# Moving checks, row loads and row sums within a two-stream graph network kernel

## The chip, the cores and the metric

One core of a Trainium2 chip. The metric is the device time of one launch in microseconds; three runs of the kernel before gave 1787.79, 1788.79 and 1789.32, median 1788.79.

## The reference

16 graphs of 1024 nodes with 128 features each. `adj` is a symmetric 0/1 matrix per graph. Two residual blocks follow each other: four layers of a gated graph network, then four layers of a graph convolution with a normalization over all graphs.

```python
h = relu(layernorm(x))
for i in range(4):                       # block 1, per graph
    m = einsum('bjn,bjd->bnd', adj, h @ weight[i])
    h = gru_cell(m, h, w_ih[i], w_hh[i], b_ih[i], b_hh[i])
x = x + h * mask[:, :, None]
h = relu(layernorm(x))
for i in range(4):                       # block 2
    h = relu(einsum('bnm,bmc->bnc', adj, h @ W[i]) + b[i])
    h = gamma[i] * (h - mean(h)) * rsqrt(var(h) + eps) + beta[i]   # over graphs and nodes
x = x + h
```

The fast path of the kernel is exact only if the low 16 bits of each element of `adj` are zero (an element then fits bf16). The kernel therefore looks at these bits of every row of `adj` and branches to a general path if any is set.

## The kernel before, in words

**Block 1.** Two streams, `sa` (even graphs) and `sb` (odd graphs), alternate. Their order is written out by hand: under a manual schedule each engine executes its instructions in the order in which the program gives them. `half_step(one, two)` does one layer of both halves of the work: the gates of stream `two` (`products`, `reset_gate`, `candidate`, `update_gate`, `less`, `mixed`, each for the node halves 0 and 1) and the aggregation of stream `one` (`agg_step`, 32 matmuls of 128x512 from 8 row tiles and a high and a low part of the features, `ghw`). In the gates, ScalarE computes `r` (L1011), VectorE applies it (L1012, L1013), ScalarE computes the tanh (L1016) and `z` (L1020), VectorE mixes (L1027 to L1034), and the result leaves by a block transpose (L720) and DMAs on SP's queue (L591) to come back as the next layer's features (L598). After the aggregation ScalarE copies the two banks of `pm` to `m` (L955); the next half step's second product reads `m`. A clock counts the half steps (the first is step 3). `at(n, place, go)` puts a piece of side work into an agenda, and `due(place)` runs it when step n reaches that place. Places stand in this order in a half step: `ins`, `start`, (gates of half 0) `beside0`, `mid`, (gates of half 1) `beside1`, `outs`, `gap`, `end`. `plan(n)` fills the agenda for a change of graphs that ends at step n: the tail of the old graph, and the load, sums, factors and blocks of the coming x (`next_load`, `next_sums`, ...).

**A change of graphs.** In its last layer a stream fetches the next adjacency, eight row tiles of 128x1024 f32 through four staging tiles that both streams share. `fetch` issues the loads of rows 0 to 3 on SP's queue (L572); `first_four` casts them to row tiles on GpSimd (L577); `last_four` glances at rows 0 to 3, then issues the loads of rows 4 to 7 into the same four tiles and casts these. A glance (L586) is a ScalarE copy of the low 16 bits with an accumulator output; a look (L610) is a VectorE maximum over the same bits. Stream `sa` looks at rows 4 to 7 at the start of the next step, ahead of the gates' VectorE work; stream `sb` glances at them in the next step's gap. A staging tile can be loaded again only when its cast and its glance or look are done. Stream `sa` changes at steps 8, 16, ..., 56, and `sb` one step later.

GpSimd also casts each row to bf16 for a DMA transpose (L615, L616) whose results go to DRAM as the transposed adjacency (L629), and issues the loads of x (L539) and the stores of the middle results (L752, L755). `mids` lets GpSimd wait for the first column of a step's new `h` (L1091) before these stores.

**Block 2.** Here a scheduler orders the instructions by its own costs and priorities. For each layer and graph, eight rows of the transposed adjacency come back (L1308), are widened to f32 by VectorE or ScalarE (L1311, L1313) and enter 32 matmuls (L524). Graph 0 of the later layers goes a different way: it aggregates features that are not normalized yet, and `raw_weights` adds the shift times the row sums of `adj[0]` (`degree`, a tile of 128x1024 in which each partition holds the same row). `row_sums` computes `degree` after graph 0 of the first layer with 16 products with a matrix of ones (L1407) and two copies (L1411).

Of the kernel before, what the change touches and what calls it, by code (L numbers as in the profile page):

```python
# [341 lines left out]
def exact_path(  # L342
# [39 lines left out]
    def tmp(name):  # L382
        return ps_t.tile([P, HALF], F32, tag="tmp", name=name)

    adjT_d = [dram.tile([NB, P, N], BF16, tag=f"adjT{b}", name=f"adjT_d{b}") for b in range(B)]
    xmid_d = [dram.tile([N, C], F32, tag=f"xmid{b}", name=f"xmid_d{b}") for b in range(B)]
    ymid_d = [dram.tile([P, N], F32, tag=f"ymid{b}", name=f"ymid_d{b}") for b in range(B)]
# [20 lines left out]
    nc.vector.memset(eps_t, EPS)  # L408
    ones = const.tile([P, 1], F32, tag="ones", name="ones")
    nc.vector.memset(ones, 1.0)  # L410
    low = const.tile([P, (B + 2) * NB], F32, tag="low", name="low")
    nc.vector.memset(low, 0.0)

# [119 lines left out]
    with ExitStack() as st:  # L533
# [46 lines left out]
        def glance(b, stage, js):  # L580

            junk = work.tile([P, N], BF16, tag="junk", name=f"junk{b}_{js[0]}", bufs=1)
            for j in js:
                lows = stage[j % 4].bitcast(U16).rearrange("p (n t) -> p n t", t=2)[:, :, 0]
                k = b * NB + j
                nc.scalar.activation(junk, lows, AF.Copy, accum_out=low[:, k : k + 1])  # L586

        def exchange_out(t, name, d=None):
            if d is None:
# [180 lines left out]
        class Stream:  # L770
# [54 lines left out]
            def plan(self, n, tail=None):  # L825

                if tail:
                    b, xt, hT, parts = tail
                    end = {}

                    def sums():
                        end["norm"] = tail_sums(b, xt, hT, parts)

                    def blocks(hf):
                        if hf == 0:
                            end["y"] = y_mid(b)
                        norm_blocks(xt, end["y"], end["norm"], range(hf * BH, (hf + 1) * BH))

                    at(n + 2, "gap", sums)
                    at(n + 3, "mid", lambda: store_xmid(b, xt))  # L840
                    at(n + 3, "gap", lambda: norm_factors(end["norm"]))
                    at(n + 4, "beside0", lambda: blocks(0))
                    at(n + 4, "beside1", lambda: blocks(1))
                    at(n + 5, "mid", lambda: store_ymid(b, end["y"]))
                if self.b + 2 < B:
                    at(n + 5, "mid", self.next_load)
                    at(n + 6, "start", self.next_sums)
                    at(n + 6, "gap", self.next_factors)
                    at(n + 7, "beside0", lambda: self.next_blocks(0))
                    at(n + 7, "beside1", lambda: self.next_blocks(1))  # L850
                    at(n + 7, "end", self.ins_away)

            def fetch(self):

                if self.i == 3 and self.b + 2 < B and not written[0]:
                    if self is sa:
                        t = turned_tile(f"stage{self.b + 2}").bitcast(F32)
                        room[0] = [t[:, 2 * q : 2 * q + 2, :].rearrange("p a n -> p (a n)") for q in range(4)]
                    self.stage = room[0]
                    stage_rows(self.b + 2, self.stage, range(4))  # L860

            def first_four(self):
                if self.stage:
# [2 lines left out]
            def last_four(self):  # L866
                if self.stage:
                    b, stage, self.stage = self.b + 2, self.stage, None
                    glance(b, stage, range(4))
                    stage_rows(b, stage, range(4, NB))  # L870
                    self.rows += round_rows(b, stage, range(4, NB))

                    def looks():
                        for j in range(4, NB):
                            look(b, stage[j % 4], j)

                    if self is sa:
                        at(clock[0] + 1, "start", looks)
                    else:
                        at(clock[0] + 1, "gap", lambda: glance(b, stage, range(4, NB)))  # L880

            def take(self):
                self.xt, self.y = self.next_x, self.next_y
# [175 lines left out]
        def at(n, place, go):  # L1059
            agenda.setdefault((n, place), []).append(go)  # L1060

        def due(place):
            for go in agenda.pop((clock[0], place), ()):
                go()

        def first_step(one, two, gated, halfway):

            feed.next_step()
            if one is sa:
                feed.jobs = transposes([(s.b, s.rows) for s in (sa, sb)])  # L1070
            one.split_step()
            feed.some(2)
            two.gate_step(0)
            two.half_away(0)
            if feed.full or (clock[0], "mid") in agenda:
                mids(two)
            feed.some(1)
            two.gate_step(1)
            two.half_away(1)
            gated()  # L1080
            one.agg_step(0)
            halfway()
            feed.some(NB if one is sa else 1)
            one.agg_step(1)
            two.finish()
            clock[0] += 1
# [8 lines left out]
        def half_step(one, two, gated=None, halfway=None):  # L1095

            feed.next_step()
            counts = (2, 1, 1)
            if one is sb and one.i == 0:
                feed.jobs = transposes([(s.b, s.rows) for s in (sa, sb)])  # L1100
                counts = (0, 0, 0)
            elif two is sb and two.i == 0:
                counts = (2, 2, 1)
            elif two is sa and two.i == 1 and two.across:
                counts = (3, 1, 1)
            due("ins")
            due("start")
            if one.i > 0:
                one.halves_back()
            else:  # L1110
                one.hw = hw_tiles(one.b, f"ghw{one.b}_0")
            two.fetch()
            feed.some(counts[0])
            two.products(0)
            two.reset_gate(0)
            due("beside0")
            two.candidate(0)
            two.less(0)
            one.high(0)
            two.update_gate(0)  # L1120
            one.low(0)
            two.mixed(0)
            two.half_away(0)
            two.first_four()
            if feed.full or (clock[0], "mid") in agenda:
                mids(two)
            one.high(1)
            feed.some(counts[1])
            two.products(1)
            two.reset_gate(1)  # L1130
            due("beside1")
            one.low(1)
            two.candidate(1)
            two.less(1)
            two.update_gate(1)
            two.last_four()
            two.mixed(1)
            two.half_away(1)
            due("outs")
            due("gap")  # L1140
            due("end")
            if gated:
                gated()
            one.agg_step(0)
            if halfway:
                halfway()
            feed.some(counts[2])
            one.agg_step(1)
            two.finish()
            clock[0] += 1  # L1150
# [4 lines left out]
        with tc.manual_schedule(engines=every):  # L1155
# [115 lines left out]

            sa.plan(0)
            sb.plan(1)
            first_step(sa, sb, looks, lambda: ahead(1))
            first_step(sb, sa, lambda: turn_ih(prep, w_g, 2), lambda: ahead(2))
            written[0] = False
# [122 lines left out]
            nc.tensor.matmul(pc[hf], w_c[:, i, :], mt[:, cols], start=True, stop=True)  # L1399
        conv_done(0, i, pc, stats)  # L1400

    def row_sums(rows):

        pd = [tmp(f"pt_deg{hf}") for hf in range(NH)]
        for j in range(NB):
            for hf in range(NH):
                nc.tensor.matmul(  # L1407
                    pd[hf], ones_r, rows[j][:, hf * HALF : (hf + 1) * HALF], start=(j == 0), stop=(j == NB - 1)
                )
        for hf in range(NH):  # L1410
            nc.scalar.copy(degree[:, hf * HALF : (hf + 1) * HALF], pd[hf])  # L1411

    xo = []

    def pieces(b):
# [28 lines left out]
            for n0, n in pieces(k):  # L1444
                nc.gpsimd.dma_start(xo_piece(k, n0, n), by_node(xmid_d[k], n0, n))

    ones_r = work.tile([P, P], F32R, tag="ones_r", name="ones_r", bufs=1)
    nc.vector.tensor_copy(ones_r, ones.to_broadcast([P, P]))
    degree = w_mT.rearrange("p l c -> p (l c)")[:, :N]

    stats = small.tile([P, B * NH, 6], F32, tag="bn_st", name="stats0")
# [1 line left out]
    for b in range(B):  # L1453
        rows = load_adjT(b, 0)
        hw_next = first_split(b + 1) if b + 1 < B else None
        pm = banks(b, 0)
        aggregate(pm, hw, rows, 0)
        if waiting:
            last = first_weights(*waiting, stats)
            if b == 1:  # L1460
                with tc.issue_after(last.ins):
                    sb.rest()
        if b == B - 1:
            hw_next = raw_split(1)
        aggregate(pm, hw, rows, 1)
        if b == 0:
            row_sums(rows)
        hw, waiting = hw_next, (b, pm)


# [112 lines left out]
```

## Time and profile before

| What | us |
|---|---|
| median of three runs | 1788.79 |
| profiled execution | 1789.26 |
| its span, first to last instruction | 1787.5 |
| TensorE busy | 1759.3 |
| VectorE busy | 1305.9 |
| ScalarE busy | 1107.6 |
| GpSimd busy | 379.3 |
| glances, 84 on ScalarE (L586) | 88.6 and 15.8 for the accumulator reads |
| looks at staged rows, 36 on VectorE (L610), one | 1.22 |
| row-sum products, 16 on TensorE (L1407) | 3.9 |
| ScalarE idle until `pm` is aggregated, before the copies to `m` | 163.5 |
| ScalarE idle until VectorE has `r`, before the tanh | 253.1 |

The granted clock of TensorE is 0.999. A line of the timeline has the start, the duration, engine, line of the kernel, operation, tiles (out<-in) and shape; "x2" means that two records are merged, and in brackets stands how long the engine sat idle before it and what ended that. A group's line has its count, busy time, mean ns of one and the idle time before it. Ends of matmuls are modelled; the distance of two starts is the sounder figure. Block 1 ends near 1166 us, block 2 near 1758.

### The profile page before, as it was taken

To read this page: it belongs to the slowest core of one execution; us is meant where nothing else is said; L and a number is where in the kernel's file an instruction comes from. 1 tells how busy PE (TensorE), PEld (TensorE's weight loads), DVE (VectorE), ACT (ScalarE), POOL (GpSimd) and SP (SyncE) were. 2 spreads that over 40 slices of the span, in tenths; PEclk is the share of its full clock that TensorE was granted. 3 is DMA by queue.
4 is the path that set the end of the run, shared out by engine and by line. 5 is a ranking of instruction groups with operands and counts; after the bars stand their busy time and mean duration, and the time that the engine had idled before them with its cause. 6 is when DMAs were issued, how large, how long until landed. Compare 5 with 4: busy or idle time off the path is not lost. (4 is left out here: it accounts for less than half of the span.)

```text
span 1787.5 us, 22335 instructions
## 1 busy us (share of the span) xinstructions
PE 1759.3 (98%) x6734; PEld 1191.7 (67%) x6734; DVE 1305.9 (73%) x2310; ACT 1107.6 (62%) x1713; POOL 379.3 (21%) x417
## 2 busy tenths in 40 slices
PE   9999999999999999999999999999999999999997
PEld 6565655565656565556555556577778888888886
DVE  7677877887887787887797787676666666666665
ACT  5356556556566556665655655476777767768765
POOL 4314323332331331422432333010100000000011
PEclk9999999999999999999999999999999999999999
DMA  7467657777676676776756768788766575767667
GB/s 259 135 175 262 189 163 272 179 208 241 204 200 213 223 212 197 245 202 202 260 169 186 265 174 227 256 287 311 271 228 241 207 253 201 245 224 245 238 217 268
DMA packets 363617, 400.16 MB, mean 224 GB/s; under 512 B 158188, under 2 KB 239888, under 8 KB 363488
## 3 DMA queue, kind: packets, MB, share of 16 engines
q1 hardware_dynamic: 342736, 323.59, 57.6%
q0 software_dynamic: 20224, 74.80, 11.3%
q8 instruction: 55, 0.90, 0.2%
q14 instruction: 74, 0.61, 0.1%
q10 hardware_dynamic: 528, 0.26, 0.0%
HBM read 267.47 MB, written 97.52 MB: 204 GB/s over the span
## 5 line engine op out<-in xcount | busy, mean ns | idle before, releaser
L524 PE MATMUL pm<-row,ghw 128*128 128x512 f32 x2048 | 503.6, 402 | 0.7 <-DVE ghw L926 0.6
L524 PEld LDWEIGHTS pm<-row,ghw 128*128 128x128 f32 x2048 | 383.8, 188 | 106.6 <-issue 29.2
L1016 ACT ACTIVATE r<-r,vecs 128x512 f32<-128x512 f32 x128 | 92.6, 723 | 255.0 <-DVE r L1013 253.1
L524 PE MATMUL pc_m<-wide,chw 128*128 128x512 f32 x1024 | 245.3, 395 | 0.0
L615 POOL CAST half<-row 128x1024 bf16<-128x1024 f32 x128 | 147.4, 1161 | 361.1 <-DMA adjT<-half 347.9
L524 PEld LDWEIGHTS pc_m<-wide,chw 128*128 128x128 f32 x1024 | 190.4, 188 | 41.9 <-issue 3.8
L524 PE MATMUL pc_g_r<-wide,chw 128*128 128x512 f32 x464 | 186.9, 403 | 0.3 <-ACT chw L501 0.3
L524 PE MATMUL pc_g_z<-wide,chw 128*128 128x512 f32 x464 | 181.0, 390 | 0.0
L577 POOL CAST row<-stage 128x1024 fp32r<-128x1024 f32 x112 | 128.6, 1156 | 243.7 <-DMA stage<-in_adj_dram 232.2
L1012 DVE SCALAR_TENSOR_TENSOR r<-g_hn,vecs,r 128x512 f32<-128x512 f32 x128 | 93.3, 729 | 117.9 <-ACT r L1011 66.9
L955 ACT COPY m<-pm 128x512 f32<-128x512 f32 x128 | 68.4, 585 | 163.5 <-PE pm L524 163.5
L1313 DVE CAST wide<-block 128x1024 fp32r<-128x1024 bf16 x160 | 109.9, 692 | 75.5 <-PE pc_m L524 48.3
L1313 DVE CAST wide<-packed 128x1024 fp32r<-128x1024 bf16 x160 | 110.1, 691 | 71.9 <-PE pc_g_z L524 53.5
L1311 ACT CAST wide<-packed 128x1024 fp32r<-128x1024 bf16 x96 | 100.6, 1048 | 58.5 <-PE pc_m L524 29.7
L993 PE MATMUL g_r<-m,w_mT 128*128 128x512 f32 x256 | 132.0, 597 | 3.4 <-ACT m L955 2.9
L1311 ACT CAST wide<-block 128x1024 fp32r<-128x1024 bf16 x96 | 100.7, 1049 | 53.9 <-PE pc_g_z L524 27.7
L993 PE MATMUL g_z<-m,w_mT 128*128 128x512 f32 x256 | 130.7, 592 | 0.0
L993 PE MATMUL g_xn<-m,w_mT 128*128 128x512 f32 x256 | 130.7, 592 | 0.0
L1361 DVE BATCH_NORM_STATS2 stats<-feat 128x6 f32<-128x512 f32 x128 | 84.1, 686 | 47.0 <-ACT feat L1360 45.9
L1029 DVE TENSOR_TENSOR h<-h,r 128x512 f32<-128x512 f32 x96 | 83.8, 872 | 41.9 <-ACT r L1016 41.8
L1033 DVE TENSOR_TENSOR h<-h,z 128x512 f32<-128x512 f32 x128 | 107.8, 842 | 6.8 <-ACT z L1020 0.2
L1011 ACT ACTIVATE r<-g_r,brz 128x512 f32<-128x512 f32 x128 | 87.9, 686 | 39.1 <-PE g_r L993 38.8
(186 smaller groups left out, 2830.5 us busy)
## 6 DMA issues: line engine op xcount, KB each, us to landing
block<-adjT_d SPq DMA_DIRECT2D x256, 256.0 KB, 4.7
packed<-adjT_d SPq DMA_DIRECT2D x256, 256.0 KB, 5.5
stage<-in_adj_dram SPq DMA_DIRECT2D x120, 512.0 KB, 5.7
adjT_d<-adjT POOLq DMA_DIRECT2D x16, 2048.0 KB, 7.7
cross_h<-t_h SPq DMA_DIRECT2D x92, 256.0 KB, 2.2
n_h<-cross_h SPq DMA_DIRECT2D x368, 64.0 KB, 2.0
xmid_d<-x POOLq DMA_DIRECT2D x16, 512.0 KB, 6.9
y<-ymid_d POOLq DMA_DIRECT2D x16, 512.0 KB, 5.4
```

Of the source, the lines that this page charges most:

```text
L524: nc.tensor.matmul(pm[hf], hw[s][:, j * P : (j + 1) * P], rows[j][:, hf * HALF : (hf + 1) * HALF], start=(j == 0 and s == 0), stop=(j == N ...
L577: nc.gpsimd.tensor_copy(t, stage[j % 4])
L615: nc.gpsimd.tensor_copy(t, row.bitcast(F32))
L993: nc.tensor.matmul(po, wT[:, i, g * C : (g + 1) * C], rhs, start=start, stop=stop)
L1011: nc.scalar.activation(r, pr, AF.Sigmoid, bias=brz[:, 3 * i : 3 * i + 1])
L1012: nc.vector.scalar_tensor_tensor(r, phn, b_hn(i), r, ALU.add, ALU.mult)
L1016: nc.scalar.activation(self.r, self.r, AF.Tanh, bias=b_in(self.i))
L1029: nc.vector.tensor_sub(ho, hin, self.r)
L1033: nc.vector.tensor_mul(ho, ho, self.z)
L1311: nc.scalar.copy(r, t)
L1313: nc.vector.tensor_copy(r, t)
L1361: nc.vector.bn_stats(stats[:, b * NH + hf, :], dst)
```

## The change

It moves side work of a change of graphs and computes the row sums elsewhere. (1) `fetch` loads two rows, and a new `fetch_more` the other two, between the reset gate and the candidate of half 0. (2) `last_four` no longer glances at rows 0 and 1; a new `first_glances` does, between the reset gate and the candidate of half 1. (3) The looks of `sa` stand two at `start` and two at a new place `looks` after `beside0`; the four late glances of `sb` stand two at `beside1` and two at `gap`. (4) The coming x is loaded at a new place `late`, after `beside1`, of step n+4, not at `mid` of step n+5. (5) A function `row_sums` on ScalarE copies each row of graph 0 with an accumulator output, at eight places of steps 5 to 8; GpSimd stores the 128x8 sums to DRAM in step 9 and, in graph 2 of block 2's first layer, loads them to all partitions of `degree`. The products with ones go. The order of SP's queue in block 1 stays as it was.

```diff
+    degree_d = dram.tile([N], F32, tag="degree", name="degree_d")
...
+    by_row = const.tile([P, NB], F32, tag="by_row", name="by_row")
...
+        def row_sums(rows, js):
+
+            for j in js:
+                junk = work.tile([P, N], BF16, tag="junk", name=f"summed{j}", bufs=1)
+                nc.scalar.activation(junk, rows[j].bitcast(F32), AF.Copy, accum_out=by_row[:, j : j + 1])
...
-                    at(n + 5, "mid", self.next_load)
+                    at(n + 4, "late", self.next_load)
...
-                    stage_rows(self.b + 2, self.stage, range(4))
+                    stage_rows(self.b + 2, self.stage, range(2))
+
+            def fetch_more(self):
+                if self.stage:
+                    stage_rows(self.b + 2, self.stage, range(2, 4))
...
-                    glance(b, stage, range(4))
+                    glance(b, stage, range(2, 4))
                     stage_rows(b, stage, range(4, NB))
                     self.rows += round_rows(b, stage, range(4, NB))
 
-                    def looks():
-                        for j in range(4, NB):
-                            look(b, stage[j % 4], j)
-
                     if self is sa:
-                        at(clock[0] + 1, "start", looks)
+                        for place, js in (("start", (4, 5)), ("looks", (6, 7))):
+                            at(clock[0] + 1, place, lambda js=js: [look(b, stage[j % 4], j) for j in js])
                     else:
-                        at(clock[0] + 1, "gap", lambda: glance(b, stage, range(4, NB)))
+                        for place, js in (("beside1", (4, 5)), ("gap", (6, 7))):
+                            at(clock[0] + 1, place, lambda js=js: glance(b, stage, js))
+
+            def first_glances(self):
+                if self.stage:
+                    glance(self.b + 2, self.stage, range(2))
...
             two.half_away(1)
+            due("late")
             gated()
...
             due("beside0")
+            due("looks")
+            two.fetch_more()
             two.candidate(0)
...
             due("beside1")
+            two.first_glances()
+            due("late")
             one.low(1)
             two.candidate(1)
...
+            for n, place, js in (
+                (5, "beside1", (0,)),
+                (6, "beside0", (1,)),
+                (6, "beside1", (2,)),
+                (6, "gap", (3,)),
+                (7, "gap", (4, 5, 6)),
+                (8, "start", (7,)),
+            ):
+                at(n, place, lambda js=js: row_sums(sa.rows, js))
+            at(9, "mid", lambda: nc.gpsimd.dma_start(degree_d.rearrange("(j p) -> p j", p=P), by_row))
...
-    def row_sums(rows):
-
-        pd = [tmp(f"pt_deg{hf}") for hf in range(NH)]
-        for j in range(NB):
-            for hf in range(NH):
-                nc.tensor.matmul(
-                    pd[hf], ones_r, rows[j][:, hf * HALF : (hf + 1) * HALF], start=(j == 0), stop=(j == NB - 1)
-                )
-        for hf in range(NH):
-            nc.scalar.copy(degree[:, hf * HALF : (hf + 1) * HALF], pd[hf])
...
-        if b == 0:
-            row_sums(rows)
+        if b == 2:
+            nc.gpsimd.dma_start(degree, degree_d.partition_broadcast(P))
```

More of the change, by code (lines that the diff above doesn't have):

```diff
@@ L1445, in fetch_x @@
                 nc.gpsimd.dma_start(xo_piece(k, n0, n), by_node(xmid_d[k], n0, n))
-    ones_r = work.tile([P, P], F32R, tag="ones_r", name="ones_r", bufs=1)
-    nc.vector.tensor_copy(ones_r, ones.to_broadcast([P, P]))
     degree = w_mT.rearrange("p l c -> p (l c)")[:, :N]
```

## The prediction

> **What bounds the kernel now.** I read the page first. TensorE is busy nearly throughout, so only what removes work from it, or waits in front of it, can count.
>
> ```profile
> PE 1759.3 (98%) x6734; PEld 1191.7 (67%) x6734; DVE 1305.9 (73%) x2310; ACT 1107.6 (62%) x1713; POOL 379.3 (21%) x417
> ```
>
> The chain of waits shows only the last 20 us, so I read TensorE's timeline instead. A half step is 12 gate products (two records each) and 32 aggregation matmuls. I take its length from one first `g_r` to the next. "S" is that start below.
>
> ```profile
> 992.89 1.02 PE L993 MATMUL g_r<-h,w_hhT 128*128 128x512 f32 x2
> ...
> 1010.46 1.02 PE L993 MATMUL g_r<-h,w_hhT 128*128 128x512 f32 x2
> ...
> 1018.66 1.12 PE L993 MATMUL g_hn<-h,w_hhT 128*128 128x512 f32 x2 [1.17 <-DVE r L1012]
> ...
> 1021.31 1.13 PE L993 MATMUL g_z<-h,w_hhT 128*128 128x512 f32 x2 [0.66 <-ACT z L1020]
> ...
> 1030.41 1.02 PE L993 MATMUL g_r<-h_in,w_hhT 128*128 128x512 f32 x2
> ...
> 1048.36 1.02 PE L993 MATMUL g_r<-h_in,w_hhT 128*128 128x512 f32 x2
> 1050.14 1.12 PE L993 MATMUL g_r<-m,w_mT 128*128 128x512 f32 x2 [0.75 <-ACT m L955]
> ...
> 1066.96 1.02 PE L993 MATMUL g_r<-h,w_hhT 128*128 128x512 f32 x2
> ```
>
> 992.89 to 1010.46 is 17.57 us, a step without a wait; most steps have exactly this length. Three per change of batches don't: here 19.95, 17.95 and 18.60. Over the seven changes (S = 150.96, 293.36, 436.95, 580.12, 725.09, 866.78, 1010.46) the first is 19.07, 19.95, 19.65, 19.64, 18.33, 19.02, 19.95; the second 17.89 to 17.95; the third 17.57, 17.89, 17.69, 18.65, 17.57, 18.87, 18.60. Above 17.57 that is 12.6 + 2.5 + 3.9 = 18.9 us. VectorE's timeline shows the cause of the first:
>
> ```profile
> 1010.72 1.22 DVE L610 TENSOR_REDUCE low<-stage 128x1 f32<-128x1024 uint16 x1 [1.08 <-DMA stage<-in_adj_dram]
> 1013.15 1.22 DVE L610 TENSOR_REDUCE low<-stage 128x1 f32<-128x1024 uint16 x1 [1.22 <-DMA stage<-in_adj_dram]
> 1015.29 1.22 DVE L610 TENSOR_REDUCE low<-stage 128x1 f32<-128x1024 uint16 x1 [0.92 <-DMA stage<-in_adj_dram]
> 1016.73 1.22 DVE L610 TENSOR_REDUCE low<-stage 128x1 f32<-128x1024 uint16 x1 [0.22 <-DMA stage<-in_adj_dram]
> 1017.87 0.74 DVE L1012 SCALAR_TENSOR_TENSOR r<-g_hn,vecs,r 128x512 f32<-128x512 f32 x1
> ```
>
> Four looks wait for row landings at the queue's head; the gate's L1012 stands behind them, so the bank of `g_hn` comes free only after 1018, then `z`'s. ScalarE's timeline shows the cause of the other two:
>
> ```profile
> 1004.74 0.73 ACT L1016 ACTIVATE r<-r,vecs 128x512 f32<-128x512 f32 x1 [2.50 <-DVE r L1013]
> ...
> 1043.73 0.73 ACT L1016 ACTIVATE r<-r,vecs 128x512 f32<-128x512 f32 x1 [5.22 <-DVE r L1013]
> ...
> 1048.46 1.06 ACT L586 ACTIVATE junk<-stage 128x1024 bf16<-128x1024 uint16 x1
> 1049.42 0.19 ACT L586 ACTIVATION_READ_ACCUMULATOR junk<-stage 128x1 f32 x1
> 1049.52 1.05 ACT L955 COPY m<-pm 128x512 f32<-128x512 f32 x2
> ```
>
> The copies of `m` should start near 1048.4; the fourth glance holds them until 1049.52. Yet ScalarE idles 2.50 and 5.22 us ahead of the tanh.
>
> **What the Trainium skill says.** (1) "TensorE: Matmul & The Clock Gate", Architectural detail: the queues of ScalarE and VectorE are strictly in order. The trace agrees: L1012 above stands behind looks that it doesn't need. (2) "ScalarE: Activation LUTs", What ACT_TABLE_LOAD costs: an activation with immediates takes 186 ns + 0.833 ns an element, 1039 ns at 1024. The glance of 1024 elements, the nearest row for a row sum, takes 1055, and its accumulator read 188; the next glance starts 1.18 us after the last, and I use that. The same page (Table sets) has copy in every set, and the glances between sigmoids indeed show no table load. (3) "GPSIMD Engine Reference", Key points: GpSimd shares its SBUF interfaces with VectorE instructions that have two SBUF inputs. The trace agrees: L1033 and L1034 take 1.52 and 1.41 us beside GpSimd's casts from 999.28 on, 0.69 elsewhere. (4) "DMA: Bandwidth & Descriptors", Rules for kernel authors: a strided last dimension makes one descriptor per element. The trace has no such transfer.
>
> **The change, part by part.**
>
> Row sums. Removed from TensorE, at 1178.3, in a stretch where it never waits:
>
> ```profile
> L1407 PE MATMUL pt_deg<-wide,ones_r 128*128 128x512 f32 x16 | 3.9, 396 | 0.0
> ```
>
> That is 3.9 us off the path, and two copies of 0.58 off ScalarE. Its neighbours must not be late instead: the copies of `cm` must precede the product that follows. They now stand behind the last cast of `wide` plus one of the next batch; 1175.0 (end of the wait for the old weights) + 1.0 + two casts of 1.0 puts the first copy's end near 1178.6, and the product comes at about 1178.9. Tight, no cost taken; 0 to 1 us late is possible. Added on ScalarE: eight activations of 1.24 us. Four stand ahead of a tanh where ScalarE idles 2.20, 1.82 and 2.84 us or at the end of step 6 (3.97 idle); three in a gap of 4.39 idle (3.6 needed); the last moves the sigmoid at 135.7 by 1.2, still ahead of its reader's need at 140.2. Nothing. If a place weren't free, 1.2 us once. The store of the sums is 1024 elements of 4 bytes, once; GpSimd's store of `xmid`, 1024 runs of 512 bytes, takes 0.89 us of its queue. The row cast queued behind it waits for its landing anyway. Its packets could hold the row loads of one change by 0 to 2 us; I take 0. The load back, one broadcast on GpSimd's queue, waits for the last use of three layers' weights at about 1130, ahead of loads that waited to 1139: nothing.
>
> First stream's change. Two glances move ahead of the tanh: 1002.3 + 2 x 1.18 = 1004.7, just when its input is ready (1004.74); in the earliest change the idle is 1.60, so the tanh slips 0.8 there, and its result leaves the core by DMA, no product waits. Rows 4 and 5 can then be loaded at about 1003.5 and 1004.7, not 1007.15 and 1008.33; rows 6 and 7 after glances ending 1007.1 and 1008.3, not 1009.4 and 1010.6. SP's order is unchanged, but all it holds behind these loads (one `pair_out`, two `pair_in`, four `h_in`, the other stream's rows) goes 2.4 us earlier. From issue to look the last row took 6.0 us (1010.70 to 1016.73), so it lands by about 1014.3. Looks 4 and 5 end by S+2 (VectorE is free at 1009.6), L1012 and L1013 run at S+2.7 to S+4.2 as in an undisturbed step, looks 6 and 7 fill S+4.2 to S+6.7. `g_hn`'s bank is free at S+3.5, needed at S+6.9; `z`'s read at S+6.6, needed at S+8.6. The 12.6 us go.
>
> What is late next: two looks (2.4 us) now stand in front of `h`, `ghw` and the second half. Five operations, a transpose, L1012, L1013 and the second `ghw` follow: S+6.7 + 4 x 0.7 + 0.7 + 1.4 + 0.7 = S+12.3. The fifth aggregation row needs it at S+10.3+3.8 = S+14.1. GpSimd's four casts of the other stream's rows fall in that stretch, and up to four operations then take 0.75 more: S+15.3. So 0 to 1.2 us per change; I take 0.4, seven times 0.4 = 2.8.
>
> Second stream's change. Its rows 0 and 1 need looks 4 and 5 and SP's turn: 2.4 earlier than 1016.79, landing before S+10 (they took 5.6); glances to S+11.5, where the tanh is ready at about S+11.5. Rows 2 and 3 land before the present S+15.6; the fourth glance ends by S+16.8, under 17.57. In the step after, glances 4 and 5 fill the 5.22 idle, and only 2.36 of glances follow `z` at 1044.9: 1047.3, ahead of 1048.4. So 2.5 + 3.9 go.
>
> Coming x, on GpSimd: one issue of 0.89 us a change, about one step (17 us) earlier, its wait for the old x's last reader included. VectorE waited 12.8 us in all for x, none of it before a product. It delays one cast ahead of a transpose whose GpSimd waits are up to 16.9: nothing, 0 to 0.5 a change.
>
> Sum: -3.9 - 12.6 - 2.5 - 3.9 + 2.8 = -20.1. The profiled execution is 1789.26 (span 1787.5, 1.8 around it), 0.5 above the median of 1788.79; from the median 1768.7.
>
> **Rivals.** (A) Forecast, 1764.5 to 1773. (B) VectorE's second `ghw` costs its 1.2 in full, or as much elsewhere: 1788.8 - 22.9 + 8.4 = 1774; 1773 to 1777. For it: 1.41 to 1.52 beside casts. Against: rows landing late in the stretch miss it. (C) Rows 6 and 7 still land late, and the looks hold VectorE in the new place: the 12.6 stay, 1788.8 - 3.9 - 6.4 = 1778.5; 1777 to 1785.2. Against: 1.7 us in hand. (D) The relief only uncovers the same waits elsewhere, within 0.2% (what a measurement here can tell from no change). (E) Slower: the second stream's glances now stand ahead of the tanh and `z` on an in-order queue; if rows 0 to 3 land late, ScalarE stands still and `m` is late in every change. It decides from 22.9/7 = 3.3 us late, the fourth row landing at S+19.6 instead of today's S+15.6. At 5 us later than today: 17.57 is passed by 4.2, 7 x 4.2 = 29 us, 1795. Against it: loads are issued earlier, not later.
>
> **Chances.** A 0.62, B 0.18, C 0.12, D 0.03, E 0.05. The range 1764.5 to 1777 holds A and B, 0.80; its low end is all 22.9 and a stray wait of 0.9 in the step at 636.34 gone, less 0.5 for the scatter of the runs. Faster 0.92, same 0.03, slower 0.05.
>
> **What would show it.** Right: no `pt_deg`; first steps near 18.0, second and third at 17.57; looks without DMA waits; copies of `m` that wait for TensorE. B: TensorE waits for `ghw` in mid-aggregation. C: waits for L1012 stay. E: waits of glances for `stage`, `m` late. A new wait of over 0.5 us in every change that isn't named here would make the prediction wrong.

## The result, and the profile after

The changed kernel took 1801.29 us, median of five runs (1797.81 to 1804.09), against 1788.82 us (1787.79 to 1790.83) for the kernel before on the same chip: ratio 1.0067, 95% interval 1.0048 to 1.0085. It is slower by 12.5 us where the forecast had it faster by 20.1, at 1764.5 to 1777. The profiled execution took 1798.23 us, with a span of 1796.5.

The savings that the forecast worked out are there. The first part of the page:

```profile
PE 1756.4 (98%) x6718; PEld 1192.5 (66%) x6718; DVE 1277.5 (71%) x2309; ACT 1115.9 (62%) x1727; POOL 371.6 (21%) x418
```

Three of ScalarE's groups of instructions (busy us and mean ns of one, then the idle time ahead of them and what ended it):

```profile
L588 ACT ACTIVATE junk<-stage 128x1024 bf16<-128x1024 uint16 x84 | 88.4, 1053 | 16.6 <-DMA stage<-in_adj_dram 14.6
L1030 ACT ACTIVATE r<-r,vecs 128x512 f32<-128x512 f32 x128 | 92.4, 722 | 155.6 <-DVE r L1027 153.6
...
L933 ACT CAST ghw<-n_h 128x512 fp32r<-128x512 f32 x92 | 55.9, 608 | 50.8 <-DMA n_h<-cross_h 50.8
```

The 16 products of `pt_deg` are gone (6734 to 6718). ScalarE's idle time ahead of the tanh, in which the moved glances now run, fell from 253.1 to 153.6. The last line is the new one: the casts of `ghw` (line 933; 919 before) wait 50.8 us in all for `n_h`, and waited 6.1 before.

TensorE's timeline over the same change of batches as in the prediction (matmul line 993 is now 1007):

```profile
1006.19 1.02 PE L1007 MATMUL g_r<-h,w_hhT 128*128 128x512 f32 x2
...
1023.77 1.02 PE L1007 MATMUL g_r<-h,w_hhT 128*128 128x512 f32 x2
...
1041.34 1.02 PE L1007 MATMUL g_r<-h_in,w_hhT 128*128 128x512 f32 x2
...
1058.91 1.02 PE L1007 MATMUL g_r<-h_in,w_hhT 128*128 128x512 f32 x2
...
1076.49 1.02 PE L1007 MATMUL g_r<-h,w_hhT 128*128 128x512 f32 x2
```

Every step is 17.57 or 17.58 now; these three were 19.95, 17.95 and 18.60. Over all seven changes only 0.33 us is left of the 18.9. VectorE's looks no longer wait for landings: here they run as two pairs around the gate's operations.

```profile
1022.68 2.30 DVE L618 TENSOR_REDUCE low<-stage 128x1 f32<-128x1024 uint16 x2
1026.62 0.75 DVE L1026 SCALAR_TENSOR_TENSOR r<-g_hn,vecs,r 128x512 f32<-128x512 f32 x1 [1.63 <-PE g_hn L1007]
1027.47 0.69 DVE L1027 TENSOR_TENSOR r<-g_xn,r 128x512 f32<-128x512 f32 x1
1028.08 2.33 DVE L618 TENSOR_REDUCE low<-stage 128x1 f32<-128x1024 uint16 x2
```

What came instead is in steps that had no wait before: steps 13, 21, 29, 37, 45, 53 and 61 (the fourth after the first step of each change) take 20.33, 23.26, 21.20, 20.33, 23.67, 23.01 and 19.33 us, 28.1 us above 17.57 in all, and step 5 takes 2.1 more than before. In step 45, which starts at 801.36, the timelines of GpSimd, of SP's queue, of ScalarE and of TensorE read:

```profile
797.72 0.89 POOL L637 DMA_DIRECT2D adjT_d<-adjT  x1 [3.68 <-DMA adjT<-half]
798.59 0.89 POOL L760 DMA_DIRECT2D xmid_d<-x  x1
799.47 0.89 POOL L541 DMA_DIRECT2D x<-in_x_dram  x1
...
799.24 9.39 SPq L606 DMA_DIRECT2D n_h<-cross_h  x8
...
812.97 0.62 ACT L933 CAST ghw<-n_h 128x512 fp32r<-128x512 f32 x1 [6.23 <-DMA n_h<-cross_h]
813.49 0.68 ACT L1034 ACTIVATE z<-g_z,brz 128x512 f32<-128x512 f32 x1
...
814.23 1.67 PE L1007 MATMUL g_z<-h,w_hhT 128*128 128x512 f32 x2 [4.12 <-ACT z L1034]
```

(`SPq` is a DMA issue on SP's queue.) GpSimd issues three transfers back to back, 2 MB, 512 KB and 512 KB. SP's eight small loads of `n_h`, 64 KB each, are issued from 799.24 on. The cast waits for `n_h`, `z` stands behind the cast, and TensorE waits 4.12 us for `z`'s bank. The same step in the kernel before, which starts at 796.49:

```profile
789.67 0.89 POOL L629 DMA_DIRECT2D adjT_d<-adjT  x1 [0.91 <-DMA adjT<-half]
790.55 0.89 POOL L752 DMA_DIRECT2D xmid_d<-x  x1
...
796.58 4.60 SPq L598 DMA_DIRECT2D n_h<-cross_h  x8
...
801.77 0.60 ACT L919 CAST ghw<-n_h 128x512 fp32r<-128x512 f32 x1
```

Two things differ. The load of `x` is in the burst, which is an edit of the change. And the store of `adjT` is issued 3.6 us ahead of the step, not 6.8, because it waits for the last transpose; nothing in the diff touches that. The view of the tile `n_h` around this step gives the landing times: first before, then after.

```profile
DMA to landing us min/median/max: 1.8/2.0/3.0
```

```profile
DMA to landing us min/median/max: 5.5/7.7/10.7
```

### The profile page after: what moved, and what is told of

Its sections match the earlier page's. It is cut to its first block, busy times and chain, and to the rows that moved or that the text cites. A ratio compares the mean times of both kernels' runs of the same rounds, so it can differ in the third digit from the quotient of the medians.

```text
span 1796.5 us, 22294 instructions
## 1 busy us (share of the span) xinstructions
PE 1756.4 (98%) x6718; PEld 1192.5 (66%) x6718; DVE 1277.5 (71%) x2309; ACT 1115.9 (62%) x1727; POOL 371.6 (21%) x418
## 3 DMA queue, kind: packets, MB, share of 16 engines
q0 software_dynamic: 20400, 75.33, 12.5%
## 5 line engine op out<-in xcount | busy, mean ns | idle before, releaser
L526 PEld LDWEIGHTS pm<-row,ghw 128*128 128x128 f32 x2048 | 386.1, 189 | 109.0 <-issue 30.7
L623 POOL CAST half<-row 128x1024 bf16<-128x1024 f32 x128 | 142.0, 1121 | 414.4 <-DMA adjT<-half 399.4
L1030 ACT ACTIVATE r<-r,vecs 128x512 f32<-128x512 f32 x128 | 92.4, 722 | 155.6 <-DVE r L1027 153.6
L1007 PE MATMUL g_z<-h,w_hhT 128*128 128x512 f32 x192 | 99.5, 600 | 22.8 <-ACT z L1034 22.8
L1043 DVE TENSOR_TENSOR h<-h,r 128x512 f32<-128x512 f32 x96 | 75.8, 789 | 46.3 <-ACT r L1030 46.2
```

What stands on the lines that cost most here:

```text
L526: nc.tensor.matmul(pm[hf], hw[s][:, j * P : (j + 1) * P], rows[j][:, hf * HALF : (hf + 1) * HALF], start=(j == 0 and s == 0), stop=(j == N ...
L623: nc.gpsimd.tensor_copy(t, row.bitcast(F32))
L1007: nc.tensor.matmul(po, wT[:, i, g * C : (g + 1) * C], rhs, start=start, stop=stop)
L1030: nc.scalar.activation(self.r, self.r, AF.Tanh, bias=b_in(self.i))
L1043: nc.vector.tensor_sub(ho, hin, self.r)
```

## The experiments

Times are medians in us. The kernel before, run beside each group, took 1790.4, 1790.2, 1792.8, 1790.3 and 1791.2; so a difference of under 3 us between groups says little.

**Group 1: which edit.** Four kernels hold the edits singly or in pairs: the load of `x` (X), the row sums on ScalarE (R), and glances, looks and row loads (G).

```diff
 e1_x_back (G+R)        after:  -at(n + 4, "late", self.next_load)  +at(n + 5, "mid", self.next_load)
 e2_x_alone (X)         before: the same line the other way, and due("late") in its two places
 e3_sums_back (G+X)     after:  without row_sums on ScalarE, degree_d, by_row; pt_deg as before
 e4_looks_alone (G)     e1 with the edit of e3
```

x back: 

> The changed kernel with only the load of the coming x put back to its old place (a step later, in the middle). Theory T1 (the moved x load puts 512 KB more on the DMA engines right behind the store of the turned adjacency, so the loads of n_h land late, the cast of ghw waits for them at the head of ScalarE's queue, z stands behind it and TensorE waits for z's bank): the waits in steps 13, 21, 29, 37, 45, 53 and 61 and in step 5 go, 28.1 + 2.1 us, and the time is 1801.3 - 30 = 1771 (1769 to 1774). Rival T2 (the steps freed of their waits make the transposes and the store of the turned adjacency later against the step, and that store alone is what collides with n_h): at most a third of the waits goes, 1791 to 1800.

x alone: 

> The kernel before with only the load of the coming x moved, as in the change; glances, looks, row loads and row sums as before. T1: the same waits for n_h ahead of z appear in steps 13 to 61, 20 to 30 us in all: 1809 to 1819. T2: the store has its old place and is drained before n_h is loaded; no new wait, 1787 to 1791. If both are needed: between, near 1797.

sums back: 

> The changed kernel with the row sums back on TensorE; x, glances, looks and row loads as changed. T1 and T2 alike: 3.9 us of products back, less at most 1.1 of a wait for cm: 1801.3 + 3 to 4 = 1804.5. Rival T3 (the sums on ScalarE cause the wait in step 5, 2.1 us): 1802 to 1803, with step 5 at 18.7 us again.

looks alone: 

> The kernel before with only the glances, looks and row loads of the change (x load in its old place, row sums on TensorE). T1: all 18.9 us of the waits at a change of batches go and nothing else is late: 1788.8 - 18.9 = 1770, plus up to 3 for a second ghw: 1770 to 1774. T2: the waits for n_h ahead of z are there without the x load: 1785 to 1796.

| kernel | edits | us | ratio, 95% |
|---|---|---|---|
| e4_looks_alone | G | 1771.1 | 0.9893 (0.9879 to 0.9908) |
| e3_sums_back | G+X | 1774.0 | 0.9905 (0.9891 to 0.9919) |
| e1_x_back | G+R | 1783.1 | 0.9959 (0.9944 to 0.9974) |
| e2_x_alone | X | 1793.0 | 1.0016 (1.0008 to 1.0023) |
| changed kernel | G+X+R | 1801.3 | 1.0067 (1.0048 to 1.0085) |

All theories missed e3: 1802 to 1804.5 was expected, 1774.0 came. They missed e1 and e2 as well; only e4 came as T1 had it. Moving `x` costs 2.6 us on the kernel before and 2.9 on G, not 20 to 30. The row sums, which take 3.9 us off TensorE, made G slower by 12.0. T1 (`x` alone) and T2 (the relief alone) both fall. The queue part of the page shows where to look; first e4, then e1:

```profile
q1 hardware_dynamic: 342736, 323.59, 58.0%
q0 software_dynamic: 20224, 74.80, 11.5%
```

```profile
q1 hardware_dynamic: 342736, 323.59, 61.0%
q0 software_dynamic: 20400, 75.33, 12.6%
```

SP's queue moves the same packets and bytes, yet they took 61.0% of 1778.9 us, 1085 us per engine, against 58.0% of 1769.3, 1026. The average packet took longer, by 59 us per engine in all, although the row sums are done by step 9 of some 64. In the view of DMA issues, the 128 transposes of the whole run, of e4 and of e1:

```profile
adjT<-half SPq DMA_TRANSPOSE x128, 2.8
```

```profile
adjT<-half SPq DMA_TRANSPOSE x128, 3.3
```

What lasts for the whole run is where the tiles lie. `by_row` is 32 bytes a partition, laid out ahead of the large tiles: in the compiled program the first `half` starts at byte 178,688 before (a multiple of 512) and at 178,720 after. `degree_d`, 4 KB, shifts tiles in DRAM likewise.

**Group 2: the shift or the sums.**

```diff
 f1_sums_64 (after)      -by_row = const.tile([P, NB], ...)   +by_row = const.tile([P, 2 * NB], ...)
                         and the store takes by_row[:, :NB]
 f4_x_back_64 (e1)       the same
 f2_pad_32 (e4)          +pad = const.tile([P, NB], F32, ...)        +nc.vector.memset(pad, 0.0)
 f3_pad_dram (e4)        +spare_d = dram.tile([N], F32, ...)         +one store of zeros to it
```

64 bytes: 

> The changed kernel with the tile of the row sums 64 bytes long instead of 32 (eight unused columns). Nothing else changes but the addresses: every tile laid out after it in SBUF then starts on a multiple of 64 bytes again, as in the kernel before; the DRAM tile of the sums stays. Theory T4 (32 bytes of by_row put nearly all later SBUF tiles 32 bytes off a 64 byte boundary, which makes the packets of the DMA transposes, loads and stores slower all through the run: with the sums on ScalarE the packets of 256 bytes took 24.0 and 23.3 ns against 20.3 to 21.4 without): about 1774.0 - 3.9 = 1770 (1767 to 1773). Rival T5 (the 4 KB of degree_d in DRAM shift the DRAM tiles behind it): no change, 1801. Rival T3 (the eight activations and the store of the sums themselves): no change, 1801.

pad of 32 bytes: 

> The changed glances, looks and row loads alone (1771.1, x and row sums as before) with an unused tile of 32 bytes a partition ahead of the later SBUF tiles, set to zero once. No row sum on ScalarE, no store of sums. T4: 1783 + 3.9 = 1787 (1782 to 1792), with the packets of 256 bytes at 23 to 24 ns. T5 and T3: 1771.

pad in DRAM: 

> The changed glances, looks and row loads alone (1771.1) with an unused DRAM tile of 4 KB ahead of the turned adjacencies, written once at the start with zeros; SBUF addresses as in the kernel before. T4 and T3: 1771 (1770 to 1773). T5: 1783 to 1790.

64 bytes and x back: 

> The changed kernel with the row sums in 64 bytes and the load of x in its old place. T4: 1771.1 - 3.9 = 1767 (1766 to 1769), the sum of the forecast without its 2.8 for the second ghw. T5, T3: as with 32 bytes, 1783.

The pad of 32 bytes, with no row sum anywhere, took 1785.8: 14.7 more than e4, with transposes at 3.3 us. The pad in DRAM took 1770.5. So the shift in SBUF is enough for the cost, and the DRAM address adds nothing; group 3 shows whether the sums' work does. T4 had this pad right. But 64 bytes did not mend it (1800.8, and 1782.0 with `x` back): the multiple that counts is larger than 64.

**Group 3: no shift, and which multiple.** g1 and g2 keep `by_row` and give back its 32 bytes elsewhere, so that all later tiles have the addresses of before.

```diff
 g1_sums_unshifted (after), g2_x_back_unshifted (e1)
-    eps_t = const.tile([P, 1], F32, tag="eps", name="eps_t")
-    ones = const.tile([P, 1], F32, tag="ones", name="ones")
+    pair = const.tile([P, 2], F32, tag="eps", name="eps_ones")
+    eps_t, ones = pair[:, :1], pair[:, 1:]
 g3_pad_128, g4_pad_256 (e4): f2's pad with 4 * NB and 8 * NB columns
```

unshifted: 

> The changed kernel, with the two constants eps and one put into one tile of 32 bytes, so that the 32 bytes of by_row shift nothing: every later SBUF tile has the address of the kernel before (most at multiples of 512 bytes). No other instruction changes. Theory T6 (the shift of the SBUF tiles, by 32 or 64 bytes alike, is the cost: the 32 byte pad alone cost 1785.8 - 1771.1 = 14.7 us): the glances and x and the row sums are left, 1774.0 - 3.9 = 1770 (1767 to 1773), the packets of 256 bytes back near 21 ns. Rival T3 (the eight activations, the store and the load of the sums): 1795 to 1801. If the shift and the sums each cost half: 1786.

unshifted, x back: 

> The same with the load of x in its old place: glances, looks, row loads and row sums of the change, no tile shifted. T6: 1771.1 - 3.9 = 1767 (1766 to 1769), faster than both kernels. T3: near 1783.

128 bytes: 

> The changed glances, looks and row loads alone (1771.1), with an unused tile of 128 bytes a partition ahead of the later tiles (32 bytes cost 14.7 us). If a start on a multiple of 128 bytes is what counts: 1771. If it takes 256 or 512 bytes: 1783 to 1790.

256 bytes: 

> The same with 256 bytes. If a start on a multiple of 128 or 256 bytes is enough: 1771. If only a multiple of 512 will do, or the addresses of before are good for another reason: 1783 to 1790.

T6 held. g1 took 1771.8 (ratio 0.9883, 0.9866 to 0.9900): the given change without the shift is faster, not slower, so the sums' work is not the cost. g2 took 1767.6 (0.9858, 0.9843 to 0.9873), the fastest of all. 128 bytes cost 11.0 over e4 (1782.1, just under the forecast for that case), 256 bytes nothing (1770.7). Of the shifts tried, 32, 64 and 128 bytes cost 11 to 15 us, 0 and 256 none. The trace's packets of the 16 engines, by size and queue (duration of one in ns):

| packets | G (e4) | +256 (g4) | +32 (f2) | +128 (g3) | half alone (h2) | adjT alone (h1) |
|---|---|---|---|---|---|---|
| 256 B, SP's queue: the transposes, mean | 20.9 | 20.4 | 24.7 | 24.0 | 24.1 | 20.9 |
| 4096 B, GpSimd's queue, median | 159 | 159 | 171 | 172 | 159 | 168 |
| 4096 B, SP's queue: row loads, median | 159 | 159 | 159 | 159 | 159 | 159 |

"DMA: Bandwidth & Descriptors", How a descriptor splits into AXI transactions, leads one to expect something of the kind: a descriptor that doesn't start on a multiple of 256 bytes begins with a transaction from the boundary below it. By it 256 bytes become two transactions instead of one and 4096 seventeen instead of sixteen, 6% more as an estimate. GpSimd's packets fit: they took 7.5% longer here (159 to 171). The transposes' packets fit less well. Their median is 18 ns in all six columns; what grew is the share of those over 20 ns, from 2% (e4, g4, h1) to about 18% (f2, g3, h2). So the page's account is not shown to be the cause. The row loads, whose destination in SBUF is shifted in f2 and g3, show none of it, nor do the transposes' packets where only their destination is shifted (h1). In these rows, what is seen to slow are packets read from a shifted tile.

**Group 4: which tile, and the shift without the change.**

```diff
 h1_turned_off (e4)        adjT's tile 256 bytes longer, its rows begin 128 bytes into it
 h2_half_off (e4)          both half tiles 128 bytes longer; rows begin at 128 and, one tile on, at 0
 h3_early_tiles_off (e4)   g3's pad, and adjT's tile 128 bytes longer with its rows 128 bytes into it
 h4_before_pad_32 (before) f2's pad
```

adjT: 

> The changed glances, looks and row loads alone (1771.1), with only the turned adjacency adjT started 128 bytes off a multiple of 256: its tile is 256 bytes longer and the rows begin 128 bytes into it, so no other tile loses its multiple of 256. The transposes write it in runs of 256 bytes and its store reads it in packets of 4096. Theory T7 (the transposes' and the store's packets on adjT are what the shift slows): most of the 11 to 15 us of a shift of everything, 1780 to 1786, with queue 0's packets at 171 and the packets of 256 bytes at 24 ns. If it is half, the source of the transposes, or the other tiles: 1771.

half: 

> The same with only the two half tiles (what the transposes read) started 128 bytes off, all else on multiples of 256. T7: 1771, with the packets of 256 bytes near 21 ns. If the transposes' reads are what is slowed: 1780 to 1786.

early tiles: 

> The same with the tiles laid out ahead of adjT (constants, weights, x, the n_h tiles) 128 bytes off and adjT, half and all later tiles on multiples of 256. T7: 1771 to 1773. If n_h's or x's own transfers are what is slowed: 1776 to 1786.

before: 

> The kernel before with an unused tile of 32 bytes ahead of the later SBUF tiles: the shift without the change. If the shift costs by itself, whatever the steps: 1790 + 11 to 15, 1801 to 1806. If it costs only because the steps freed of their waits leave the DMA engines no room (T2 in a new form): 1790 to 1795.

The packets answer as the table shows: `half`, the transposes' source, carries all of the transposes' slowing, `adjT` most of the slowing of GpSimd's packets. The times don't follow: 1771.7, 1772.2 and 1773.0, each within e4's interval. T7 falls: neither alone costs what the whole shift does. The kernel before loses too, 8.4 us (1798.7; ratio 1.0041, 1.0026 to 1.0056), so the freed steps aren't needed for it; but that lies between both forecasts, and G loses 14.7 to the same pad.

Step 45 shows why one part alone can be free. The store of `adjT` in e4 and in h2, and then the cast of `ghw` in h2, the same cast in f2, and TensorE's wait in f2 (the step starts at 784.99, 785.08 and 791.52):

```profile
778.10 0.89 POOL L629 DMA_DIRECT2D adjT_d<-adjT  x1 [0.63 <-DMA adjT<-half]
```

```profile
780.94 0.89 POOL L629 DMA_DIRECT2D adjT_d<-adjT  x1 [3.50 <-DMA adjT<-half]
...
791.79 0.62 ACT L925 CAST ghw<-n_h 128x512 fp32r<-128x512 f32 x1 [1.33 <-DMA n_h<-cross_h]
```

```profile
799.65 0.62 ACT L927 CAST ghw<-n_h 128x512 fp32r<-128x512 f32 x1 [2.75 <-DMA n_h<-cross_h]
...
800.91 1.12 PE L1001 MATMUL g_z<-h,w_hhT 128*128 128x512 f32 x2 [0.64 <-ACT z L1028]
```

With slow transposes alone (h2) the store is issued 4.1 us ahead of the step instead of 6.9, and the cast waits 1.33 us, but TensorE does not wait. With all tiles shifted (f2) the cast waits 2.75 us and TensorE 0.64; in the changed kernel, with `x` in the burst too, 6.23 and 4.12.

**Group 5: the rest of the tiles, and the last link.**

```diff
 i1_later_tiles_off (e4)   adjT's tile 128 bytes longer, rows at its start; half as in h2 (on multiples of 256 again)
 i2_z_ahead_of_ghw (after)
-            one.high(0)
             two.update_gate(0)
+            one.high(0)
             one.low(0)
```

later tiles: 

> The changed glances, looks and row loads alone (1771.1), with the tiles laid out behind adjT (h, rows, staging of the exchanges in and out) 128 bytes off, and adjT, half and all tiles ahead of adjT on multiples of 256. Shifts of adjT, of half and of the early tiles alone cost 0.6, 1.1 and 1.9 us; a shift of all cost 11.0. If the costs add: 1771.1 + 11.0 - 3.6 = 1778.5, with the packets of 512 bytes above 30 ns. If they don't add, since a wait appears only where several queues are late together: 1771.5 to 1774.

z first: 

> The changed kernel as it was given (tiles shifted, x load moved) with one edit of order: z is issued to ScalarE ahead of the first cast of ghw in every half step, instead of behind it. If the waits in steps 13 to 61 are z standing behind a cast that waits for n_h: no wait of TensorE for z's bank is left there; TensorE waits at the start of the aggregation for ghw itself instead, about 2 us less in each of seven steps (example: step 45 ends its gates at S + 10.1 and ghw would be there at S + 12.2), so 1801 - 14 = 1787 (1782 to 1793). If z's wait has another cause (its input, the granted clock): 1798 to 1803.

i1 took 1771.4. The packets of 512 bytes on SP's queue took 30.7 ns in the mean, against 28.8 in e4, and still the time did not move. The four parts alone cost 0.6, 1.1, 1.9 and 0.3, 3.9 together and each under the 3 us that groups differ by, against 11.0 for all at once (g3). The costs don't add.

i2 took 1800.8 (1.0066, 1.0042 to 1.0090): not the 1787 of the forecast. TensorE waits 0.6 us for `z` in the whole run, not 23.4, and the time is the same within the scatter. Its TensorE timeline in step 45:

```profile
814.04 3.15 PE L526 MATMUL pm<-row,ghw 128*128 128x512 f32 x7 [2.73 <-ACT ghw L933]
```

Most of the wait has gone to the aggregation, which needs the late `ghw` itself: 14.8 us in the whole run. `n_h` is what is late; the place of `z` in the queue only decides where the wait shows. The 14 us of the forecast also left out the clock. The view of windows has the granted clock in the column after POOL. The changed kernel in step 45, up to the wait's end and after it:

```profile
801.36:814.20 12.84, 8.75 (x21) 3.61 (x19) 2.72 (x4) 6.50 (x12) 1.02 (x2) 1.00 1.08 274
814.20:825.03 10.83, 10.80 (x37) 7.58 (x38) 10.05 (x26) 3.94 (x9) 4.14 (x6) 0.84 0.69 191
```

and i2:

```profile
814.00:823.30 9.30, 9.26 (x33) 7.20 (x34) 8.83 (x18) 4.10 (x9) 4.40 (x6) 0.82 0.87 207
```

A finer cut of the changed kernel shows what the 0.84 is a mean of:

```profile
814.68:818.09 3.41, 3.41 (x6) 1.59 (x5) 3.24 (x5) 2.12 (x6) 2.76 (x4) 0.50 0.11 42
818.09:825.03 6.94, 6.94 (x32) 5.69 (x32) 6.33 (x21) 1.33 (x3) 1.17 (x3) 1.00 0.94 258
```

Half the clock for 3.41 us loses an estimated 1.7 us on top of the wait of 4.12. The changed kernel has three such stretches, after the waits of 3.77, 4.12 and 3.52 us in steps 21, 45 and 53. i2 has four, each after a wait of only 2.73 to 2.85 us (steps 13, 29, 45 and 61). "TensorE: Matmul & The Clock Gate", Part 1, has the clock halved after an idle window of some 3.4 us. The measurement decides: i2's shorter waits were enough, while one of 3.35 us in step 29 of the changed kernel brought no such stretch, so the length of a wait alone doesn't settle it. The stretches of one run start at whole multiples of 3.413 us from each other (in the changed kernel 381.18, 814.68 and 961.45, which is 127 and 43 of them), so where a wait falls on that raster seems to count as well; no run tests it. Shorter waits didn't save the clock here.

## Why the prediction was wrong

**What bounds the kernel, and the two kinds of waits: right.** G alone gave 19.3 us (1790.4 to 1771.1) against 12.6 + 2.5 + 3.9 in the forecast. The steps show the 18.9 us gone.

**The 2.8 us for VectorE's second `ghw`: too much.** TensorE waits 0.2 us for it in the whole run. That fits the argument against rival B; no run tests the reason by itself.

**Row sums on TensorE: right in size, and incomplete.** The 3.9 us are gone and the copy of `cm` is 0.7 late, within the 0 to 1 that was named: 3.2 net, and g2 against g4, in one group, shows 3.2 (1770.7 to 1767.6). The list of what is added is where the forecast broke. It priced eight activations, a store and a load, and put the 32 bytes of `by_row` at nothing without naming them. They shift almost every large tile of the fast path off multiples of 256 bytes: +15 us (e1 against e4 is 12.0, plus the 3.2 saved; f2 against e4 is 14.7).

**Coming x: "nothing, 0 to 0.5 a change". Wrong.** I costed GpSimd's issue of 0.89 us and the cast queued behind it, not its 512 KB on the 16 engines. The load goes into a burst that it shares with 2.5 MB of stores, straight ahead of the next step's `n_h`. "DMA: Bandwidth & Descriptors", Issuing engines are not separate DMA queues, says that transfers of all queues interleave on the same engines; the landings of `n_h` above agree. Without the shift it costs 2.6 to 4.2 us (e2, e3 against e4, and g1 against g2, where no run of one overlaps the other). With the shift it costs 18.8 (f1 against f4).

**Why the two multiply.** The kernel without the shift but with `x` moved (g1), whose step 45 starts at 788.33:

```profile
781.57 0.89 POOL L637 DMA_DIRECT2D adjT_d<-adjT  x1 [0.73 <-DMA adjT<-half]
782.44 0.89 POOL L760 DMA_DIRECT2D xmid_d<-x  x1
783.32 0.89 POOL L541 DMA_DIRECT2D x<-in_x_dram  x1
...
789.19 6.47 SPq L606 DMA_DIRECT2D n_h<-cross_h  x8
...
794.80 0.62 ACT L933 CAST ghw<-n_h 128x512 fp32r<-128x512 f32 x1 [1.09 <-DMA n_h<-cross_h]
```

The store is at 6.8 us ahead of the step again. By the packets of GpSimd's queue, 1.9 of the burst's 3 MB are through when the step starts, against 0.7 in the changed kernel, and the cast waits 1.09 us, not 6.23. With the shift the transposes take 3.3 us, the last of them ends late, and most of the burst moves onto `n_h`. With the shift and `x` in its old place (e1) the loss is smaller and in part has another form, since `x` then lands too late: VectorE's longest wait for it is 5.1 us against 3.0 in the kernel before. Step 38 of e1, VectorE then TensorE:

```profile
671.58 0.29 DVE L672 BATCH_NORM_STATS2 st_in<-x 128x6 f32<-128x128 f32 x1 [3.03 <-DMA x<-in_x_dram]
...
675.55 1.13 PE L1007 MATMUL g_hn<-h,w_hhT 128*128 128x512 f32 x2 [0.61 <-DVE r L1026]
```

The sum of the measured parts: -19.3 (G) - 3.2 (sums) + 15.2 (shift) + 18.8 (`x` under the shift) = +11.5; measured +12.5. The first three make e1 against its kernel before by the way they were taken; the last is the term that the sum tests.

**The rivals.** Rival E had the right sign and the wrong mechanism: glances wait 14.6 us for rows, and TensorE waits 0.3 us for `m` in the whole run. None of my cases held a cost that lies outside the listed instructions, and 0.05 for slower was too little. The last sentence of the prediction, that a new wait over 0.5 us in every change would make it wrong, is what happened.

**Open.** Which combination of tiles makes the 11 to 15 us isn't settled: no part alone shows it, and no two parts were shifted together. h2 shows that slow transposes alone make the store late; that the late store and the burst then hold up `n_h` is read from the timelines, as no run delayed the store by itself. Why not quite a fifth of the transposes' packets slow down isn't known. Other multiples than those of 32, 64, 128 and 256 bytes weren't tried.

## What to carry to other kernels

A small tile laid out ahead of large ones can slow the transfers of all tiles behind it. Compare the SBUF addresses of both programs; where they moved, try the tiles on multiples of 256 bytes, which cost nothing here; and read each queue's share of time at equal packets and bytes. A moved load has a price on the shared engines, not only on its queue: look at what else is in flight there, and at which small load comes next. For this kernel the version to keep is g2: glances, looks and row sums of the change, `x` in its old place, and two constants in one tile, 1767.6 us.

## What was not expected of the hardware

- With all tiles 32 bytes off, or their source alone 128 bytes off, the transposes took 3.3 us from issue to landing instead of 2.8. With all tiles 32 bytes off, GpSimd's 4096 byte packets took 171 ns instead of 159.
- A shift of each part of the tiles alone cost nothing that shows (0.3 to 1.9 us); a shift of all cost 11 to 15 us of 1771.
- After waits of 2.73 to 4.12 us TensorE had half its clock for 3.41 us in seven places, an estimated 1.7 us each, and none after one wait of 3.35 us.
